# Soft mixture-of-experts block: an expert's second product for two batches side by side in the full array, in groups of four

## Chip, cores and metric

The kernel runs on one NeuronCore of a Trainium2 chip. The metric is device time in microseconds (us) of one execution. Three timed runs of the kernel before gave 1167.07, 1167.43 and 1168.63 us; the median is 1167.43 us. All data are fp32.

## The reference

Sixteen batches of 100 tokens, width 256, pass through a cross attention (16 heads of 16, 361 context tokens each) and then through a soft mixture of 16 experts with 64 slots each. Only the second half matters here:

```python
logits  = einsum('bnd,esd->bnes', x, se)
dispatch = softmax(logits, axis=1)                 # over the tokens
combine  = softmax(logits.reshape(b, n, -1), -1)   # over all 16 * 64 slots
slots = einsum('bnd,bnes->besd', x, dispatch)
gate  = gelu(einsum('besd,edf->besf', slots, Wg) + bg)
up    = einsum('besd,edf->besf', slots, Wu) + bu
eout  = einsum('besf,efo->beso', gate * up, Wd) + bd
out   = x + einsum('bns,bso->bno', combine, eout)  # slots of all experts flattened
```

Per expert, Wg and Wu are 256x512, Wd is 512x256; each is 512 KB.

## The kernel before

**Groups.** The batches go through in groups of 2, 2, 4, 4 and 4 (`GROUPS`). For each group all weights of the 16 experts are streamed in again (80 expert passes, number k = 16 g + e), into six slots of `w_all`. `load_weights` (L1266) issues the next load of a fixed list on SyncE's queue whenever `give_back` (L1282) returns a slot, and with each Wd also that expert's bias `bd`, broadcast to 64 rows: the even expert of a pair has rows 0 to 63 of the tile `bd_bc`, the odd one rows 64 to 127.

**Attention.** `units` works batch by batch: scores (L785) and exponentials (L810) on TensorE in tiles of 32 rows, the product with the values (L833) in tiles of 32 columns, and around them VectorE and ScalarE steps (L790, L801, L818).

**Dispatch.** `dispatch_quarter(g, p, q)` (L927) takes a pair p of batches and a quarter q of the experts (four experts, 256 slots). The logits `lg` have slots on the partitions: 128 partitions are two experts of 64 slots. `copies` (L962) brings them to the tile `lg_all`; they are kept there and later become the combine weights. After the softmax over tokens, two products `sl` (L1033, one per batch) give the slots, transposed, and VectorE (i = 0, L1045) and ScalarE (i = 1, L1048) write them, scaled, into `ring`, ordered (expert, half of the width, batch, slot) by `slots_of` (L914).

**Experts.** `experts(g)` (L1322) takes expert after expert. In a group of four, T = 4*64 = 256 columns; the hidden width is worked in two parts of two 128-wide chunks. Each part makes `gp` and then `up` (L1347, stationary 128x128 weights, moving 256 slot columns, which lie in one run), ScalarE's gelu gives `ge` (L1358), and VectorE's `hT = (up + bu) * ge` (L1363). So hT has the hidden width on partitions and (chunk, batch, slot) on the columns.

**Second product.** `down(g, e, hts)` (L1287) takes a pair of experts after the first part of the expert that follows (at a group's end, at once). Per two batches it makes one PSUM bank `dn`: for each batch and each of four chunks, the stationary operand is one batch's 64 columns of hT, and the two experts of the pair stand in the two 64-column halves of the array. Rows 0 to 63 of `dn` are thus the even expert, rows 64 to 127 the odd one. One VectorE addition (L1309) over 128 partitions and 512 elements adds the bias and writes `eouts_of`, over the quarter's slots in `ring`. Then both Wd slots are returned.

**Combine.** `combine_quarter(g, q)` (L1208) makes, for each batch, `po` (L1218) as the sum over the quarter's two expert pairs c of `lg_all[.., 2c+i, :]` (stationary) and `eouts[:, c, batch, :]` (moving): 128 partitions hold the two experts' slots, and both operands need them in the same order. VectorE adds it to `acc` (L1229). It is run an expert later than it could be; at a group's end it follows the last `down` at once.

**Order.** All of it is issued in an order fixed in advance: generators yield before each step, and a planner with a model of the engines' times (`Clock`, `ck.pe`, `ck.psum_dve`, `ck.copy`) picks whichever task is ready next, with the experts behind the attention units and some of the dispatches. PSUM has four banks for all `mm_tile` products (L65 on), which are taken in turn.

Of the kernel before, what the change touches and what calls it, by code (L numbers as in the profile page):

```python
# [33 lines left out]
F32 = mybir.dt.float32  # L34
AF = mybir.ActivationFunctionType
ALU = mybir.AluOpType
# [11 lines left out]
P = 128  # L48
# [3 lines left out]
QE = 4  # L52
# [77 lines left out]
def xattn_ffn_kernel(  # L130
# [777 lines left out]
    def quarters_before(g, q):  # L908
# [2 lines left out]
        over = [r for r in range(NQ) if spans[g - 1, r][0] < a1 and a0 < spans[g - 1, r][1]]  # L911
        return max(over, default=-1) + 1

    def slots_of(g, q):  # L914
        n = GROUPS[g]
        return regions[g, q].rearrange("p (e k b s) -> p e k b s", e=QE, k=KD, b=n)

    def eouts_of(g, q):
        return regions[g, q].rearrange("p (e b d) -> p e b d", e=QE // 2, d=D)
# [7 lines left out]
    def dispatch_quarter(g, p, q):  # L927

        b0 = 2 * p

        def gate():
            if any(starts[g] + b0 + i not in out_t for i in range(2)):
                return NEVER
            if (g and combined[g - 1] < quarters_before(g, q)) or not lg_free:
                return NEVER
            return max(seT_t[q // 2], out_t[starts[g] + b0 + 1])

        yield gate, 1, (1.35, 0.6, 1.7)
        lg = mm_tile("lg")
        for c in range(2):  # L940
            for kd in range(KD):
                nc.tensor.matmul(  # L942
                    lg[:, c * 2 * N : (c + 1) * 2 * N],
                    lhsT=seT[:, kd, (2 * q + c) * P : (2 * q + c + 1) * P],
                    rhs=xnTs[g][:, kd, b0 * N : (b0 + 2) * N],
                    start=kd == 0,
                    stop=kd == KD - 1,
                )
        t = ck.pe(800, ck.bank())
        lgv = lg[:, : 4 * N].rearrange("p (c n) -> p c n", n=N)  # L950
        slot = lg_free.pop(0)
        lgs = lg_all[:, slot]
        mx = two.tile([P, 4], F32, tag="mx", name="d_mx")
        if len(exps) < 2:
            exps.append(const.tile([P, 4, P], F32, name=f"d_ex{len(exps)}"))
            nc.gpsimd.memset(exps[-1][:, :, N:], 0.0)
        exs = exps[turn[0] % 2]
        turn[0] += 1
        ex = exs[:, :, :N]
        sm = two.tile([P, 4], F32, tag="sm", name="d_sm")  # L960

        def copies(t):  # L962
            nc.scalar.copy(lgs, lgv)
            return ck.copy(400, t)

        def maxima(src, t):
            nc.vector.tensor_reduce(mx, src, AX.X, ALU.max, negate=True)
            return ck.run("DVE", 0.6, t)

        def exponentials(src, t):  # L970
            for i in range(4):
                nc.scalar.activation(
                    ex[:, i],
                    src[:, i],
                    AF.Exp,
                    bias=mx[:, i : i + 1],
                    accum_out=sm[:, i : i + 1],
                )
                t = ck.act("exp", 130, t)
            return t  # L980

        copied = g or q
        if copied:
            tl = copies(t)
            ck.free(tl)
            t = maxima(lgs, tl)
        else:
            t = exponentials(lgv, maxima(lgv, t))
            tl = copies(0.0)
            ck.free(tl)  # L990
        yield t, 0, (0.0, 0.8, 0.0)
        if copied:
            t = exponentials(lgs, t)
            yield t, 0
        nc.vector.reciprocal(sm, sm)  # L995
        t = ck.run("DVE", 0.18, t)
        late = nc.gpsimd if g else nc.vector
        late.tensor_tensor(ex, ex, sm.unsqueeze(2).to_broadcast([P, 4, N]), ALU.mult)  # L998
        t = ck.run("POOL", 0.95, t) if g else ck.run("DVE", 0.6)

        def dispatch():
            disp_sb = two.tile([P, 2, 256], F32, tag="disp", name="disp")
            disp = disp_sb[:N]
            td = t
            if g >= BY_DVE:
                src = exs.rearrange("p (c i) n -> p i c n", c=2)
                dst = disp_sb.rearrange("p i (c a s) -> p i c a s", c=2, a=4)
                for a in range(4):
                    for tb in range(4):
                        if tb % 2 == 0:  # L1010
                            yield td, 0, (0.0, 0.4, 0.0), "aside"
                        toks = slice(32 * tb, 32 * tb + 32)
                        nc.vector.transpose(  # L1013
                            dst[toks, :, :, a, :], src[32 * a : 32 * a + 32, :, :, toks]
                        )
                        td = ck.run("DVE", 0.3, t)
            else:
                tp = mm_tile("d_t")
                for c in range(2):
                    for i in range(2):  # L1020
                        nc.tensor.transpose(  # L1021
                            tp[:N, i * 256 + c * P : i * 256 + (c + 1) * P],
                            ex[:, 2 * c + i, :],
                            ident,
                        )
                nc.scalar.copy(disp.rearrange("n i s -> n (i s)"), tp[:N])
                td = ck.copy(512, ck.run("PE", 0.45, t, ck.bank()))
                ck.free(td)
            for i in range(2):
                yield td, 1, (0.87, 0.4, 0.4)  # L1030
                sl = mm_tile("sl")
                for kd in range(KD):
                    nc.tensor.matmul(  # L1033
                        sl[:, kd * 256 : (kd + 1) * 256],
                        lhsT=xns[g][:, b0 + i, kd * P : (kd + 1) * P],
                        rhs=disp[:, i, :],
                        start=True,
                        stop=True,
                    )
                t2 = ck.pe(512, td, ck.bank())  # L1040
                for kd in range(KD):
                    dst = slots_of(g, q)[:, :, kd, b0 + i, :]
                    srcv = sl[:, kd * 256 : (kd + 1) * 256].rearrange("p (e s) -> p e s", s=S)
                    if i == 0:
                        nc.vector.tensor_scalar(dst, srcv, ng_c[kd], nb_c[kd], ALU.mult, ALU.add)  # L1045
                        t2 = ck.psum_dve(256, t2)
                    else:
                        nc.scalar.activation(  # L1048
                            dst, srcv, AF.Identity, bias=nb_c[kd], scale=ng_c[kd]
                        )  # L1050
                        t2 = ck.copy(256, t2)
                ck.free(t2)
                slot_t[g, q] = max(slot_t.get((g, q), 0.0), t2)
            slots_left[g, q] -= 1
            left[g] -= 1

        yield t, int(g < BY_DVE), (0.45, 0.0, 0.6)
        yield from dispatch()

        yield tl, 0, (0.0, 0.8, 0.0)  # L1060
        if (g, p) not in tops:
            tops[g, p] = [two.tile([P, 2, N], F32, tag="top", name="top"), 0, 0.0]
        top = tops[g, p]
        if top[1]:
            nc.vector.tensor_tensor(top[0], top[0], lgs[:, 0:2], ALU.max)
            nc.vector.tensor_tensor(top[0], top[0], lgs[:, 2:4], ALU.max)
            top[2] = ck.run("DVE", 0.8, tl)
        else:
            nc.vector.tensor_tensor(top[0], lgs[:, 0:2], lgs[:, 2:4], ALU.max)
            top[2] = ck.run("DVE", 0.4, tl)  # L1070
        top[1] += 1
        logits[g, p, q] = slot
# [193 lines left out]
    def load_weights():  # L1266
# [7 lines left out]
        nc.sync.dma_start(t, src.rearrange("(k p) f -> p k f", p=P))  # L1274
        weights[k, name] = t
        if name == "wd":
            if k % 2 == 0:
                biases[k // 2] = two.tile([P, D], F32, tag="bd", name="bd_bc")
            rows = slice(S * (k % 2), S * (k % 2) + S)
            nc.sync.dma_start(biases[k // 2][rows], bd[e].partition_broadcast(S))  # L1280

    def give_back(*names):  # L1282
        for n in names:
# [3 lines left out]
    def down(g, e, hts):  # L1287
# [5 lines left out]
        for half in range(n // 2):  # L1293
            yield max(t for h in hts for _, t in h), 1
            dn = mm_tile("dn")
            for i in range(2):
# [12 lines left out]
            nc.vector.tensor_tensor(  # L1309
                eouts_of(g, q)[:, j // 2, 2 * half : 2 * half + 2, :],  # L1310
                dn.rearrange("p (b d) -> p b d", d=D),
                biases[k // 2].unsqueeze(1).to_broadcast([P, 2, D]),
                ALU.add,
            )
            t = ck.psum_dve(512, ck.pe(2048, ck.bank()))
            ck.free(t)
            done_t[g, q] = t
        give_back((k, "wd"), (k + 1, "wd"))

    HALVED = (1,)  # L1320

    def experts(g):  # L1322
# [4 lines left out]
        for e in range(E):  # L1327
# [3 lines left out]
            for part in range(FC // FB):  # L1331
# [3 lines left out]
                for kind in range(2):  # L1335
# [5 lines left out]
                    for f, fc in enumerate(fcs):  # L1341
# [4 lines left out]
                        for kd in range(KD):  # L1346
                            nc.tensor.matmul(  # L1347
                                ps[:, f * T : (f + 1) * T],
                                lhsT=w[:, kd, fc * P : (fc + 1) * P],
                                rhs=slots_of(g, q)[:, j, kd].rearrange("p b s -> p (b s)"),  # L1350
                                start=kd == 0,
                                stop=kd == KD - 1,
                            )
# [19 lines left out]
                hts.append((hT, t))  # L1373
                if part == 0:
                    if e % 2 == 0 and pair:
                        yield from down(g, e - 2, pair)
                        pair = []
                    if e % QE == 1 and e > 1:
                        to_combine.append(q - 1)
# [1 line left out]
                        yield from combine_quarter(g, to_combine.pop(0))  # L1381
            give_back((k, "wg"), (k, "wu"))
            pair.append(hts)
        yield from down(g, E - 2, pair)
        for q in to_combine + [NQ - 1]:
            yield from combine_quarter(g, q)

# [205 lines left out]
```

## Time and profile before

| | |
|---|---|
| median of three runs | 1167.43 us |
| span of the profiled execution, first to last instruction | 1165.9 us |
| profiled execution, total time apart from the span | not listed; the span is 1.5 us below the median, 1.2 us below the fastest run |
| TensorE busy / VectorE / ScalarE / GpSimd | 1151.4 / 664.6 / 569.4 / 153.7 us |
| TensorE clock granted | 1.00 in every stretch |
| DMA engines busy, data moved | 39.6% by the main queue, 144.84 MB |

The profiled execution has these stretches (us from the span's start): 0 to 97 before the first second product, 97 to 240 and 240 to 440 mostly groups 0 and 1, 440 to 766 group 2 with the attention of groups 3 and 4 in between, 766 to 973 group 3, 973 to 1166 group 4. A busy line of the profile has: source line, engine, operation, tile written <- tiles read, shapes, count, then busy us and mean ns of one, then idle time before it and what ended that. "PE" is a matmul, "PEld" a load of the stationary operand. Each fp32 product of the source is two matmul instructions in the trace. A timeline line has: start us, length us, engine, line, operation, tiles, shapes, count; in it like neighbours are merged. A matmul's length includes its way through the array (0.38 us for 256 columns), while the next one starts earlier; so rates are read from start to start.

### The profile page before, as it was taken

To read this page: it belongs to the slowest core of one execution; us is meant where nothing else is said; L and a number is where in the kernel's file an instruction comes from. 1 tells how busy PE (TensorE), PEld (TensorE's weight loads), DVE (VectorE), ACT (ScalarE), POOL (GpSimd) and SP (SyncE) were. 2 spreads that over 40 slices of the span, in tenths; PEclk is the share of its full clock that TensorE was granted. 3 is DMA by queue.
4 is the path that set the end of the run, shared out by engine and by line. 5 is a ranking of instruction groups with operands and counts; after the bars stand their busy time and mean duration, and the time that the engine had idled before them with its cause. 6 is when DMAs were issued, how large, how long until landed. Compare 5 with 4: busy or idle time off the path is not lost.

```text
span 1165.9 us, 24315 instructions
## 1 busy us (share of the span) xinstructions
PE 1151.4 (99%) x9769; PEld 893.5 (77%) x9769; DVE 664.6 (57%) x1646; ACT 569.4 (49%) x1131; POOL 153.7 (13%) x257
## 2 busy tenths in 40 slices
PE   8899999999999999999999999999999999999998
PEld 6588878787788777777777767787788878777876
DVE  5755546576644678744575765668634456544222
ACT  3556555576454757545545655564433336413110
POOL 3110121013000223300100100031200002002000
PEclk9999999999999999999999999999999999999999
DMA  5415665533467412333521421343443344345441
GB/s 135 136 39 168 204 216 165 161 103 124 140 215 235 116 56 57 72 114 114 134 80 44 119 89 37 114 128 113 136 150 130 113 150 127 114 132 171 134 129 55
DMA packets 138588, 144.84 MB, mean 124 GB/s; under 512 B 45050, under 2 KB 97228, under 8 KB 138476
## 3 DMA queue, kind: packets, MB, share of 16 engines
q1 hardware_dynamic: 137258, 141.50, 39.6%
q8 instruction: 77, 1.26, 0.4%
q0 software_dynamic: 496, 1.12, 0.3%
q10 hardware_dynamic: 722, 0.67, 0.2%
q14 instruction: 35, 0.29, 0.1%
HBM read 141.60 MB, written 1.66 MB: 123 GB/s over the span
## 4 chain that ended last, share of the span: by engine, by line
PE 95%; DVE 2%; DMA 2%; SPq 0%; issue 0%; ACT 0%; POOL 0%; DVEq 0%; ACTq 0%
PE dn L1300 20%; PE gp L1347 19%; PE up L1347 19%; PE sl L1033 5%; PE po L1218 5%; PE at L810 4%; PE at L785 4%; PE v_ps L673 4%; PE lg L942 3%; PE k_ps L613 3%; PE cx L833 3%; DVE mxp L790 1%; PE o_ps L726 1%; PE q_ps L538 1%; PE at L1400 1%; PE d_t L1021 1%
## 5 line engine op out<-in xcount | busy, mean ns | idle before, releaser
L1347 PE MATMUL gp<-ring,w_all 128*128 128x256 f32 (+1 forms) x1280 | 249.1, 341 | 0.5 <-DMA w_all<-in_L_ffn_Wg_dram 0.5
L1347 PE MATMUL up<-ring,w_all 128*128 128x256 f32 (+1 forms) x1280 | 247.9, 340 | 0.0
L1363 DVE SCALAR_TENSOR_TENSOR hT<-up,parT,ge 128x256 f32<-128x256 f32 (+1 forms) x320 | 119.2, 422 | 208.0 <-PE up L1347 157.5
L1300 PE MATMUL dn<-w_all,hT 128*64 128x256 f32 x2048 | 232.1, 382 | 0.0
L1358 ACT ACTIVATE ge<-gp,parT 128x256 f32<-128x256 f32 (+1 forms) x320 | 116.9, 429 | 230.8 <-PE gp L1347 230.1
L1347 PEld LDWEIGHTS gp<-ring,w_all 128*128 128x128 f32 x1280 | 204.5, 191 | 27.9 <-issue 7.3
L1347 PEld LDWEIGHTS up<-ring,w_all 128*128 128x128 f32 x1280 | 204.9, 191 | 21.5 <-issue 1.1
L1300 PEld LDWEIGHTS dn<-w_all,hT 128*64 128x64 f32 x2048 | 142.6, 137 | 78.0 <-issue 7.9
L790 DVE TENSOR_REDUCE mxp<-at 100x4 f32<-100x1444 f32 x64 | 106.2, 1659 | 28.5 <-PE at L785 27.8
L1309 DVE TENSOR_TENSOR ring<-dn,bd_bc 128x512 f32<-128x512 f32 x64 | 44.3, 692 | 131.1 <-PE dn L1300 130.9
L1358 ACT ACT_TABLE_LOAD x71 | 91.1, 1283 | 34.0 <-PE gp L1347 29.5
L818 ACT ACTIVATE aT<-at 121x1200 f32<-121x1200 f32 x64 | 74.9, 1170 | 37.8 <-PE at L810 34.9
L1013 DVE STREAM_TRANSPOSE disp<-d_ex 32x128 f32<-32x128 f32 x256 | 77.4, 302 | 4.6
L717 POOL TENSOR_TENSOR cxs<-cxs,rs 128x100 f32<-128x100 f32 x63 | 25.0, 396 | 381.6 <-DVE rs L714 322.3
L818 ACT ACT_TABLE_LOAD x43 | 55.2, 1283 | 24.1 <-DVE q L801 12.6
L998 POOL TENSOR_TENSOR d_ex<-d_ex,d_sm 128x400 f32<-128x400 f32 x28 | 23.9, 857 | 297.5 <-DVE d_sm L995 297.5
L1033 PE MATMUL sl<-disp,xn 100*128 100x256 f32 x256 | 62.9, 388 | 0.1
L1048 ACT ACTIVATE ring<-sl,parT 128x256 f32<-128x256 f32 x64 | 32.6, 559 | 56.6 <-PE sl L1033 56.6
L1218 PE MATMUL po<-ring,lg_all 128*100 128x256 f32 x256 | 59.7, 383 | 0.0
L810 PEld LDWEIGHTS at<-q,kT 32*121 32x121 f32 x1344 | 40.6, 180 | 19.3 <-issue 7.0
L842 ACT COPY cxs<-cx 128x100 f32<-128x100 f32 x64 | 15.6, 243 | 81.1 <-PE cx L833 80.3
L1033 PEld LDWEIGHTS sl<-disp,xn 100*128 100x128 f32 x256 | 46.7, 190 | 9.5 <-issue 2.5
(165 smaller groups left out, 1323.6 us busy)
## 6 DMA issues: line engine op xcount, KB each, us to landing
w_all<-in_L_ffn_Wg_dram SPq DMA_DIRECT2D x80, 512.0 KB
w_all<-in_L_ffn_Wu_dram SPq DMA_DIRECT2D x80, 512.0 KB
w_all<-in_L_ffn_Wd_dram SPq DMA_DIRECT2D x80, 512.0 KB
bd_bc<-in_L_ffn_bd_dram SPq DMA_DIRECT2D x80, 64.0 KB
c_sb<-in_ctx_dram SPq DMA_DIRECT2D x96, 44.0 KB
acc<-in_x_dram SPq DMA_DIRECT2D x7, 200.0 KB
out_dram<-acc SPq DMA_DIRECT2D x7, 200.0 KB
ring<-n_L_ffn_slot_embeds_dram POOLq DMA_DIRECT2D x1, 1024.0 KB, 7.7
```

The source lines that it names most:

```text
L673: nc.tensor.matmul(ps[: KC + 1, :D], lhsT=cT[:, kd, c * KC : c * KC + KC + 1], rhs=w_sb["wv"][:, kd, :], start=kd == 0, stop=kd == KD - 1,)
L785: nc.tensor.matmul(self.at[:N, r, :S2], lhsT=self.q[rows], rhs=self.k[rows], start=True, stop=True)
L790: nc.vector.tensor_reduce(mxv[:, :, m : m + 1], self.at[:N, :, :S2], AX.X, ALU.max, negate=True)
L810: nc.tensor.matmul(self.at[: KC + 1, r, c * N : (c + 1) * N], lhsT=self.k[rows, c * KC : c * KC + KC + 1], rhs=self.q2[rows], start=True, ...
L818: nc.scalar.activation(self.aT[: KC + 1], self.at[: KC + 1, :, : 3 * N], AF.Exp)
L1013: nc.vector.transpose(dst[toks, :, :, a, :], src[32 * a : 32 * a + 32, :, :, toks])
L1033: nc.tensor.matmul(sl[:, kd * 256 : (kd + 1) * 256], lhsT=xns[g][:, b0 + i, kd * P : (kd + 1) * P], rhs=disp[:, i, :], start=True, stop=True,)
L1218: nc.tensor.matmul(pos[i][:N, :D], lhsT=lg_all[:, slot, 2 * c + i, :], rhs=eouts_of(g, q)[:, c, 2 * p + i, :], start=c == 0, stop=c == 1,)
L1300: nc.tensor.matmul(dn[S * x : S * x + S, i * D : (i + 1) * D], lhsT=hts[x][fc // FB][0].rearrange("p (f b s) -> p f b s", f=FB, s=S)[:, fc ...
L1347: nc.tensor.matmul(ps[:, f * T : (f + 1) * T], lhsT=w[:, kd, fc * P : (fc + 1) * P], rhs=slots_of(g, q)[:, j, kd].rearrange("p b s -> p (b ...
L1358: nc.scalar.activation(ge[:, cols], ps[:, cols], AF.Gelu, bias=col(8, e, fc))
L1363: nc.vector.scalar_tensor_tensor(out=hT[:, cols], in0=ps[:, cols], scalar=col(NPAR, e, fc), in1=ge[:, cols], op0=ALU.add, op1=ALU.mult,)
```

## The change

It applies to groups of four only (`crossed`). Groups of two are computed as before.

- `copies`: for the second pair of batches (p = 1) the logits' upper and lower 64 partitions change places on the way to `lg_all`, with two copies of 64 partitions in place of one of 128. Everything after (softmax, dispatch, combine weights) then has the two experts of each 128 the other way round for these batches.
- The slots of a quarter lie in `ring` as (expert pair c, half of the width, y, batch in pair, slot): y = 0 and 2 are the first pair of batches' even and odd expert, y = 1 and 3 the second pair's odd and even expert. `expert_slots` reads an expert's 256 columns as (batch in pair, y, slot): four runs of 64, of which the even expert's y are 0 and 3, the odd one's 1 and 2.
- So 128 neighbouring columns of hT are one batch of each pair side by side, and for the odd expert the second pair comes first. `crossed_down` makes one bank `dn` per expert with a 128-column stationary operand; its two evictions write 64 partitions each, to where `eouts` has that expert for that pair.
- Each Wd slot is returned after its expert's products, and `bd` is broadcast to 128 rows per expert, in four tiles in place of two.

```diff
+    def crossed(g):
+        return GROUPS[g] == 4
...
+    def crossed_slots(g, q):
+        return regions[g, q].rearrange("p (c k y b s) -> p c k y b s", c=2, k=KD, y=4, b=2)
+
+    def expert_slots(g, q, j, kd):
+        if not crossed(g):
+            return slots_of(g, q)[:, j, kd].rearrange("p b s -> p (b s)")
+        own = slice(1, 3) if j % 2 else slice(0, 4, 3)
+        return crossed_slots(g, q)[:, j // 2, kd, own].rearrange("p y b s -> p b y s")
...
         def copies(t):
+            if crossed(g) and p:
+                nc.scalar.copy(lgs[:S], lgv[S:])
+                nc.scalar.copy(lgs[S:], lgv[:S])
+                return ck.copy(400, ck.copy(400, t))
             nc.scalar.copy(lgs, lgv)
             return ck.copy(400, t)
...
-                    dst = slots_of(g, q)[:, :, kd, b0 + i, :]
-                    srcv = sl[:, kd * 256 : (kd + 1) * 256].rearrange("p (e s) -> p e s", s=S)
+                    srcv = sl[:, kd * 256 : (kd + 1) * 256]
+                    if crossed(g):
+                        dst = crossed_slots(g, q)[:, :, kd, p::2, i, :]
+                        srcv = srcv.rearrange("p (c x s) -> p c x s", c=2, s=S)
+                    else:
+                        dst = slots_of(g, q)[:, :, kd, b0 + i, :]
+                        srcv = srcv.rearrange("p (e s) -> p e s", s=S)
...
         if name == "wd":
+            if crossed(k // E):
+                biases[k] = two.tile([P, D], F32, tag="bd", name="bd_bc", bufs=4)
+                nc.sync.dma_start(biases[k], bd[e].partition_broadcast(P))
+                return
             if k % 2 == 0:
-                biases[k // 2] = two.tile([P, D], F32, tag="bd", name="bd_bc")
+                biases[k] = two.tile([P, D], F32, tag="bd", name="bd_bc", bufs=4)
             rows = slice(S * (k % 2), S * (k % 2) + S)
-            nc.sync.dma_start(biases[k // 2][rows], bd[e].partition_broadcast(S))
+            nc.sync.dma_start(biases[k - k % 2][rows], bd[e].partition_broadcast(S))
...
+    def crossed_down(g, e, hts):
+        k = g * E + e
+        q, j = divmod(e, QE)
+        for x in range(2):
+            yield max(t for h in hts for _, t in h), 1
+            dn = mm_tile("dn")
+            w = weights[k + x, "wd"]
+            for i in range(2):
+                for fc in range(FC):
+                    at = (fc % 2 * 2 + i) * P
+                    nc.tensor.matmul(
+                        dn[:, i * D : (i + 1) * D],
+                        lhsT=hts[x][fc // 2][0][:, at : at + P],
+                        rhs=w[:, fc, :],
+                        start=fc == 0,
+                        stop=fc == FC - 1,
+                    )
+            t = ck.pe(2048, ck.bank())
+            for half in range(2):
+                rows = slice(S * half, S * half + S)
+                p = half ^ x
+                nc.vector.tensor_tensor(
+                    eouts_of(g, q)[rows, j // 2, 2 * p : 2 * p + 2, :],
+                    dn[rows].rearrange("p (b d) -> p b d", d=D),
+                    biases[k + x][rows].unsqueeze(1).to_broadcast([S, 2, D]),
+                    ALU.add,
+                )
+                t = ck.psum_dve(512, t)
+            ck.free(t)
+            done_t[g, q] = t
+            give_back((k + x, "wd"))
...
-                                rhs=slots_of(g, q)[:, j, kd].rearrange("p b s -> p (b s)"),
+                                rhs=expert_slots(g, q, j, kd),
...
-                        yield from down(g, e - 2, pair)
+                        yield from (crossed_down if crossed(g) else down)(g, e - 2, pair)
...
-        yield from down(g, E - 2, pair)
+        yield from (crossed_down if crossed(g) else down)(g, E - 2, pair)
```

More of the change, by code (lines that the diff above doesn't have):

```diff
@@ L1311, in down @@
                 dn.rearrange("p (b d) -> p b d", d=D),
-                biases[k // 2].unsqueeze(1).to_broadcast([P, 2, D]),
+                biases[k].unsqueeze(1).to_broadcast([P, 2, D]),
                 ALU.add,
```

## The prediction

> **What bounds the kernel now.** I read the page first: its shares, its 40 slices and its groups.
>
> ```profile
> span 1165.9 us, 24315 instructions
> PE 1151.4 (99%) x9769; PEld 893.5 (77%) x9769; DVE 664.6 (57%) x1646; ACT 569.4 (49%) x1131; POOL 153.7 (13%) x257
> ...
> PEclk9999999999999999999999999999999999999999
> ...
> L1300 PE MATMUL dn<-w_all,hT 128*64 128x256 f32 x2048 | 232.1, 382 | 0.0
> ...
> L1309 DVE TENSOR_TENSOR ring<-dn,bd_bc 128x512 f32<-128x512 f32 x64 | 44.3, 692 | 131.1 <-PE dn L1300 130.9
> ```
>
> TensorE has work 99% of the time at the full clock, in groups 2 to 4 (440 to 1166 us) idle for 0.6 us and the last 4. VectorE is busy 64, 56 and 40% in the stretches of groups 2, 3 and 4 (table of windows). So only what shortens TensorE's own sequence, or makes it wait, can move the end. The second product is 232 us of it, but the busy time can't tell what one product costs, since ends are modelled. I therefore went to the timeline of TensorE and read starts. Group 4, one `down`:
>
> ```profile
> 1131.77 1.89 PE L1347 MATMUL up<-ring,w_all 128*128 128x256 f32 x8
> ...
> 1133.59 7.13 PE L1300 MATMUL dn<-w_all,hT 128*64 128x256 f32 x64
> ...
> 1140.64 2.00 PE L1347 MATMUL gp<-ring,w_all 128*128 128x256 f32 x8
> ...
> 1142.47 1.89 PE L1347 MATMUL up<-ring,w_all 128*128 128x256 f32 x8
> ```
>
> Between full products, starts are 1.726 us apart per 8 instructions (gp at 776.11, up at 777.84, gp at 779.56): 0.216 us each. The 64 half-width `dn` instructions start in pairs, 7 ns and then 209 ns apart: again 0.216 us per pair. **The two halves of the array already run side by side, so full tiling gains nothing per column:** 32 full instructions will take the 32 x 0.216 = 6.91 us that 32 pairs take.
>
> What the half tiling does cost stands at its borders. From the first `up` (1131.77) to the second (1142.47) are 10.70 us; the work between is 8 + 32 + 8 slots of 0.2158 = 10.36. The other **0.34 us** are: 0.09 before the first `dn` (1131.77 + 1.73 = 1133.50, start 1133.59), 0.05 after its first pair (260 instead of 209 ns), 0.10 before `gp`, 0.10 after gp's first instruction (hence 2.00 instead of 1.89). None of it appears between full products.
>
> In group 2 the attention's 32-row and 32-column products stand around `dn`, and they pay borders of their own:
>
> ```profile
> 676.69 0.89 PE L810 MATMUL at<-q,kT 32*121 32x100 f32 x24
> 677.51 3.67 PE L1300 MATMUL dn<-w_all,hT 128*64 128x256 f32 x32
> 681.12 0.87 PE L785 MATMUL at<-kT,qp 32*100 32x361 f32 x8
> 681.91 0.72 PE L833 MATMUL cx<-aT,vpad 120*32 120x100 f32 x24
> 682.57 1.99 PE L1347 MATMUL gp<-ring,w_all 128*128 128x256 f32 x8
> ```
>
> Here `dn` would be a full product between two 32-row ones. Entering a full product from 32-row or 32-column work costs 0.13 or 0.11 plus 0.10 after its first instruction (this gp's 1.99), leaving it for them 0.09; `dn` now pays 0.13 or 0.11, then 0.05, then 0.10. Such a place loses 0.05.
>
> **The change, part by part.**
>
> *Borders.* I went through all 34 separate stretches of `dn` in groups 2 to 4 with these prices, neighbours as they are now:
> - full product on both sides, 18 stretches (10 in group 3, 8 in group 4): 0.345 each, 0.323 before `po`; together 3.39 + 2.75 = 6.14 us.
> - full on one side only, 13 in group 2: 0.15 each where it leads into 32-row work (9 of them, one 0.21), 0.05 to 0.10 where it comes from `cx` into a single transpose (4); together 1.76 us.
> - neither, 3 in group 2: -0.05 each, -0.14 us.
>
> Sum: **7.75 us saved**, if the order stays.
>
> *Evictions.* 24 pairs of experts had two evictions of 128 x 512; now four of 64 x 512. Partitions do not make them cheaper: additions of 200 elements take 439 ns on 128 partitions (L1066), 381 on 64 (L1156), 433 on 32 (L1157). So 48 more at 0.692 = 33.2 us of VectorE, 11.1 per group, which brings it to 67, 61 and 46% there. Inside a group these lie beside the following products; the combine that reads them comes an expert later, and `dn`'s bank is asked for again only after three other products. If that cover were gone, all 33 us would stand on the path.
>
> *Where the cover is gone: a group's end.* There `po` follows `dn` at once.
>
> ```profile
> 1151.20 7.13 PE L1300 MATMUL dn<-w_all,hT 128*64 128x256 f32 x64
> 1151.38 0.88 DVE L1363 SCALAR_TENSOR_TENSOR hT<-up,parT,ge 128x256 f32<-128x256 f32 x2 [2.58 <-PE up L1347]
> 1154.92 0.69 DVE L1309 TENSOR_TENSOR ring<-dn,bd_bc 128x512 f32<-128x512 f32 x1 [2.67 <-PE dn L1300]
> ...
> 1158.26 3.70 PE L1218 MATMUL po<-ring,lg_all 128*100 128x256 f32 x16
> 1158.38 0.69 DVE L1309 TENSOR_TENSOR ring<-dn,bd_bc 128x512 f32<-128x512 f32 x1 [2.76 <-PE dn L1300]
> ```
>
> Before, the first half's eviction was long done and `po` for the first pair of batches ran while the second half was evicted. Now both pairs of batches need the last expert's two evictions, and the first pair's comes second (for the odd expert, rows 0 to 63 are the second pair). The wait: an eviction starts 0.45 us after the last `dn` instruction starts; two in a row take about 0.61 + 0.69 (two hT in a row: 400 ns start to start at 484 each, so 84 overlap), and TensorE starts 0.055 us after (as L810 after L801): 1.81 us. Of that, 0.65 is covered: the last `dn` slot and the two `po` instructions that read the quarter's first expert pair. **1.16 us** of wait, with 14 `po` products and everything after them queued behind it on TensorE. At group 4's end nothing can fill it. At group 3's end (`dn` to `po` at 969.38 directly) I charge it in full, though the planner, which knows of the later evictions, may put dispatch products there. At group 2's end a `cx` stands between, and about 0.3 is left. Sum **2.6 us lost**.
>
> *Swapped logits.* 12 quarters (3 groups, p = 1) get a second copy: 0.49 us each (L963), 5.9 us of ScalarE at 55% and less, and 0.49 later for the maximum and all after. The slots are used a group later, and TensorE's list of waits (9.8 us in all) has no wait for slots in groups 2 to 4: nothing.
>
> *Strided slots.* gp and up now read four runs of 64 instead of one of 256, in 1536 instructions. No matmul of this trace reads more than one run. Below: 0, a gain has no reason. Above: a run priced like an instruction of its own. 128 columns take 0.112 us and 256 take 0.216, so 8 ns per start, three more starts, 24 ns: 36.9 us. The nearest rows for runs of 64 are the writers of these slots: L1048 writes 4 x 64 in 559 ns, while one-run writes with the same two column operands take 436 (100 elements, L758) and 649 (361, L639), which puts 256 at 563. No price; I take 0.
>
> *Weights and biases.* The even expert's Wd slot returns half a `down` (3.5 us) earlier; the load issues, as many as before and in the same order on SyncE, are delayed by nothing. The 48 biases grow from 64 to 128 KB, 3.1 MB on 144.84, with DMA at 31 to 41% in these groups: nothing. They are four tiles deep, two pairs, as before.
>
> *Stationary loads.* The trace shows loads of 128 columns at 0.19 us beside matmuls of 0.216 without a gap (8 gp in 1.73 us), so `dn` in this form costs no more. The Trainium skill, "TensorE: Matmul & The Clock Gate", Part 3, What overlaps and what doesn't, speaks against the change: it lets a load overlap a running matmul only if the row groups differ, which full-height loads never do. By it, 768 exposed loads of 0.19 would cost 146 us; gp and up contradict it here. "SBUF — State Buffer", Specifications (TRN2), charges reads that use too little of a 16-byte line; runs of 256 bytes use whole lines, so by it the strided read costs nothing, which no run here shows.
>
> **Sum.** 1165.9 - 7.75 + 2.6 = 1160.8 us of span, 5.1 less; the median stands 1.5 above the span, so **1162.3 us**. The planner sees one more eviction per `dn` and will order some steps differently; one border more or less is 0.2 to 0.35 us, so I allow 2.5 either way.
>
> **Rivals.**
> - *Forecast, 1159.8 to 1165.0:* borders gone, group ends paid. 0.64. With it goes the case that the planner fills the ends: up to 7.75, 1159.7; 0.06.
> - *VectorE gives it back, 1165.1 to 1169.7:* not only the ends wait. For it: VectorE works its list in the order issued and stands still behind `dn` (130.9 us of its idle time), and in group 2 the chain maximum, transpose, addition (L790, L801) runs through it; L810 already waited 3.5 us for L801. Each eviction that hits such a chain costs up to 0.61 us, 16 places in group 2 make 9.8; 5 hits (3 us) bring the change within the bound. Against: at 67% there is room, and in group 2's 326 us TensorE is idle for 0.6 in all (table of windows: busy 325.38), because the planner puts other products into such chains. Seven hits give 4.2, 1166.5; 0.18.
> - *Strided reads, slower:* at L1347, 1536 instructions. From 3.3 ns each the gain is gone, from 4.9 ns the kernel is slower by over 0.2%; at 8 ns it is 1162.3 + 12.3 = 1174.6, at 24 ns 1199. For it: no such row. Against: the writers above. 0.10.
> - *It doesn't do what it says:* `dn` still with gaps of its own, as if the 128-column loads weren't hidden. From 10 ns per instruction (768) slower. gp and up speak against it. 0.02.
>
> **Chances and range.** What a measurement of this kernel can tell from no change is about 0.2%, 2.3 us. Faster 0.64 + 0.06 = 0.70, same 0.18, slower 0.12. For 8 in 10 the range runs from 1159.5 (all borders, filled ends) to 1168.0 (most of the VectorE case); the strided case, whose bound lies far out, and a little of the VectorE case stay outside, 0.16 in all.
>
> **What would show it.** `dn` as 128*128 instructions 0.216 us apart, 768 of them in groups 2 to 4 beside 512 of the old form; in group 4 gp to up to `dn` to gp without 0.09 or 0.10 in between, and 10.36 us where 10.70 stood; gp of four runs with unchanged starts (else the strided rival); L1309 at 0.69 us for 64 partitions; a wait of about 1.2 us of `po` on VectorE's L1309 successor at the end; no growth of TensorE's waits for VectorE in group 2 (else the second case). Wrong would be the forecast if full `dn` kept a border cost, or if the waits at the ends were over 2 us each.

## The result, and the profile after

The changed kernel takes 1172.22 us (median of five runs, 1170.85 to 1173.79) against 1167.43: 1.0034 times the time before, 95% interval 1.0021 to 1.0047. It is slower by 4.8 us; the forecast was 1162.3, 5.1 faster. The profiled execution has a span of 1170.4 us, 4.5 more than before.

Page of the changed kernel (in a group line: busy us, mean ns of one, then idle time before it):

```profile
span 1170.4 us, 22908 instructions
...
PE 1148.8 (98%) x9001; PEld 934.9 (80%) x9001; DVE 697.3 (60%) x1694; ACT 560.6 (48%) x1131; POOL 153.5 (13%) x257
...
PEclk9999999999999999999999999999999999899999
...
L1358 PE MATMUL dn<-w_all,hT 128*128 128x256 f32 x768 | 171.8, 380 | 0.0
...
L1369 DVE TENSOR_TENSOR ring<-dn,bd_bc 64x512 f32<-64x512 f32 x96 | 66.1, 689 | 76.6 <-PE dn L1358 75.8
```

TensorE has 768 instructions fewer and VectorE 33 us more, as the diff says. What had not been there is the 8 in the clock's row near its end, and idle time of TensorE. The table of its waits after 440 us (engine, line and tile that waited <- what ended it: total us, times, longest):

```profile
PE sl L1051 <- DVE disp L1031: 4.6, 1, 4.6
PE po L1241 <- DVE ring L1369: 2.1, 2, 1.1
```

These are two of its three lines; the third, 0.4 us, is a wait of `q_ps` that the kernel before has too, with 0.3, as the only line of its table. The two lines shown are two different things. `po` waits for evictions at the ends of groups, as forecast. The 4.6 us are a wait for slots in group 4. TensorE's timeline there, changed kernel:

```profile
1002.63 1.89 PE L1407 MATMUL gp<-ring,w_all 128*128 128x256 f32 x8
1004.36 1.89 PE L1407 MATMUL up<-ring,w_all 128*128 128x256 f32 x8
1010.88 3.75 PE L1051 MATMUL sl<-disp,xn 100*128 100x256 f32 x8 [4.64 <-DVE disp L1031]
1014.43 2.30 PE L956 MATMUL lg<-xnT,seT 128*128 128x200 f32 x8
1016.57 1.67 PE L1407 MATMUL gp<-ring,w_all 128*128 128x256 f32 x7
```

The slots' product `sl` of the second quarter, second pair of batches, waits for VectorE's transposes of `disp`; the experts of that quarter cannot begin without it. When it does run, `sl` takes 3.75 us and `lg` 2.30. Before the change the same product came early, 12 us ahead of the `gp` that reads it (at 1012.61), and both ran at their usual lengths:

```profile
1000.89 1.89 PE L1033 MATMUL sl<-disp,xn 100*128 100x256 f32 x8
1002.62 1.52 PE L942 MATMUL lg<-xnT,seT 128*128 128x200 f32 x8
1003.97 1.89 PE L1347 MATMUL gp<-ring,w_all 128*128 128x256 f32 x8
```

The longer instructions are the clock's. Table of windows of the changed kernel, 1009.00 to 1016.02 us (PE, PEld, DVE, ACT and POOL busy, then the granted clock, 0.51, the DMA share and GB/s):

```profile
1009.00:1016.02 7.02, 5.14 (x13) 4.45 (x14) 4.50 (x15) 1.02 (x2) 0.00 (x0) 0.51 0.11 43
```

In the clock's own records it stands at 0.5 from 1009.19 for 6.83 us. From the start of `sl` to the `gp` that follows are 5.69 us; before, with the same instructions, 3.08: 2.6 us lost to the clock.

Is VectorE simply too busy to transpose in time? Its timeline says no (the time in brackets is idle time ahead of the instruction, and what ended it):

```profile
992.47 1.39 DVE L1369 TENSOR_TENSOR ring<-dn,bd_bc 64x512 f32<-64x512 f32 x2 [2.51 <-PE dn L1358]
993.89 1.24 DVE L1031 STREAM_TRANSPOSE disp<-d_ex 32x128 f32<-32x128 f32 x4
995.93 1.39 DVE L1369 TENSOR_TENSOR ring<-dn,bd_bc 64x512 f32<-64x512 f32 x2 [0.79 <-PE dn L1358]
997.35 1.25 DVE L1031 STREAM_TRANSPOSE disp<-d_ex 32x128 f32<-32x128 f32 x4
...
1002.90 0.88 DVE L1423 SCALAR_TENSOR_TENSOR hT<-up,parT,ge 128x256 f32<-128x256 f32 x2 [1.30 <-PE up L1407]
1003.81 0.62 DVE L1031 STREAM_TRANSPOSE disp<-d_ex 32x128 f32<-32x128 f32 x2
...
1009.49 1.90 DVE L1031 STREAM_TRANSPOSE disp<-d_ex 32x128 f32<-32x128 f32 x6
```

Between 988 and 1007 us VectorE idles five times for TensorE, 5.9 us in all, while transposes wait further down its list, which come two or four at a time between evictions and `hT`. The order put them there.

**Where the 4.5 us of span come from**, by comparing starts of the two traces step by step: borders -7.75 (the order is another, so this is the forecast's figure; against experiment 2 below, which has this order and the old products, they are 7.5); group ends +2.4 (1.21 twice); the late slots +4.8 of wait, from start to start, and +2.6 of clock; two waits at the end of group 1 (`d_t` for GpSimd's `d_ex` 1.1 us, `sl` for ScalarE's `disp` 0.7) +1.8; the start +0.7, among it another 3.41 us of half clock at 43 us that cost 1.6 and that two other runs, 1170.85 and 1171.02, don't have by their mean clock (0.997 against 0.995). Sum +4.55, which is the 4.5 within its rounding. The fall at 43 us is chance: both kernels run the same TensorE sequence up to 420 us. Without it the changed kernel takes about 1170.9 us, 3.5 more than before.

### The profile page after: what moved, and what is told of

It reads as the page before. It is cut to its first block, busy times and chain, and to the rows that moved or that the text cites. A ratio compares the mean times of both kernels' runs of the same rounds, so it can differ in the third digit from the quotient of the medians.

```text
span 1170.4 us, 22908 instructions
## 1 busy us (share of the span) xinstructions
PE 1148.8 (98%) x9001; PEld 934.9 (80%) x9001; DVE 697.3 (60%) x1694; ACT 560.6 (48%) x1131; POOL 153.5 (13%) x257
## 3 DMA queue, kind: packets, MB, share of 16 engines
q8 instruction: 71, 1.16, 0.4%
## 4 chain that ended last, share of the span: by engine, by line
PE 96%; DVE 2%; ACT 1%; issue 0%; DMA 0%; POOL 0%; SPq 0%; DVEq 0%; ACTq 0%
PE gp L1407 19%; PE up L1407 19%; PE dn L1358 14%; PE sl L1051 5%; PE dn L1327 5%; PE po L1241 5%; PE at L810 5%; PE at L785 4%; PE lg L956 4%; PE v_ps L673 4%; PE k_ps L613 3%; PE cx L833 3%; PE o_ps L726 1%; PE q_ps L538 1%; PE at L1460 1%; DVE mxp L790 1%
## 5 line engine op out<-in xcount | busy, mean ns | idle before, releaser
L1358 PE MATMUL dn<-w_all,hT 128*128 128x256 f32 x768 | 171.8, 380 | 0.0
L1358 PEld LDWEIGHTS dn<-w_all,hT 128*128 128x128 f32 x768 | 144.7, 190 | 20.4 <-issue 0.6
L1369 DVE TENSOR_TENSOR ring<-dn,bd_bc 64x512 f32<-64x512 f32 x96 | 66.1, 689 | 76.6 <-PE dn L1358 75.8
L1327 PE MATMUL dn<-w_all,hT 128*64 128x256 f32 x512 | 58.8, 382 | 0.0
```

What stands on the lines that cost most here:

```text
L1327: nc.tensor.matmul(dn[S * x : S * x + S, i * D : (i + 1) * D], lhsT=hts[x][fc // FB][0].rearrange("p (f b s) -> p f b s", f=FB, s=S)[:, fc ...
L1358: nc.tensor.matmul(dn[:, i * D : (i + 1) * D], lhsT=hts[x][fc // 2][0][:, at : at + P], rhs=w[:, fc, :], start=fc == 0, stop=fc == FC - 1,)
L1369: nc.vector.tensor_tensor(eouts_of(g, q)[rows, j // 2, 2 * p : 2 * p + 2, :], dn[rows].rearrange("p (b d) -> p b d", d=D), biases[k + x][r ...
```

## The experiments

The planner that fixes the order is told costs by the code: `ck.psum_dve(512, t)` for each eviction, `ck.copy(400, t)` for each copy of the logits. The diff adds a second of both. A kernel's real instructions and what the planner is told can thus be varied separately. Two theories: **ORDER**, the told costs made another order, in which the slots come late; **VECTORE**, the extra evictions themselves delay VectorE's chains, in whatever order.

**1. new_products_old_order.** The changed kernel, the planner told as before.

```diff
-                return ck.copy(400, ck.copy(400, t))
+                return ck.copy(400, t)
...
-                t = ck.psum_dve(512, t)
+                if half:
+                    t = ck.psum_dve(512, t)
```

> The changed kernel, but the planner is told what it was told before (one eviction per dn bank, one copy of the logits), so TensorE's instructions come in the order of the kernel before; all evictions and copies are still made. Theory ORDER (the loss is the order that the planner made from the new costs: the slots of group 4's second quarter come late, TensorE waits 4.6 us and then runs at half clock): borders saved 7.75, group ends lost 2.6, so about 1162.3 us (1161 to 1164), clock 1.00 from 100 us on, no TensorE wait over 1.5 us in groups 2 to 4. Theory VECTORE (the 33 us of extra evictions themselves delay what TensorE waits for): 1168 us or more, with a wait of several us on VectorE in groups 2 to 4.

1165.78 us, ratio 0.9989 (0.9980 to 0.9998), span 1164.3. TensorE's sequence is now that of before but for the `dn`, and the wait of 4.6 us is gone, as ORDER has it; yet most of the gain is missing. Its waits after 760 us:

```profile
PE po L1241 <- DVE ring L1369: 2.9, 3, 1.6
PE sl L1051 <- DVE disp L1031: 0.8, 1, 0.8
PE o_ps L726 <- DVE cxs L721: 0.6, 1, 0.6
```

With the same order, every step can be compared with before: the borders give 7.75 (1.62, 3.39 and 2.75 in groups 2, 3, 4), the three group ends take 0.39 + 1.81 + 1.21 = 3.4, and four places inside groups where TensorE now waits for VectorE take 0.50 + 0.42 + 0.86 + 0.89 = 2.7. Together -1.65. From group 2's first product to TensorE's last start the trace is 1.0 shorter, so 0.6 of smaller steps are not in this list; another 0.4 lies ahead of group 2, and the span is 1.6 shorter.

Two of these items are not the evictions'. The 0.50 stands at 449 us, ahead of group 2's first `dn`, where second copies of the logits are the only instructions that are new; the chain that ends there runs through one (L979, 0.49 us at 438.79), then the maximum `d_mx`, VectorE's list and a transfer. And at the end of group 3 the evictions come late because VectorE, which works in the order of its list, stands at a `d_mx` that waits for the second copy:

```profile
967.95 0.57 DVE L985 TENSOR_REDUCE d_mx<-lg_all 128x4 f32<-128x400 f32 x1 [4.11 <-ACT lg_all L979]
968.43 1.38 DVE L1369 TENSOR_TENSOR ring<-dn,bd_bc 64x512 f32<-64x512 f32 x2
```

They start 1.01 us after the last `dn` starts, where 0.42 pass at the end of group 4: hence 1.81 in place of 1.21.

**2. old_products_new_order.** The opposite: the kernel before, the planner told what the changed kernel tells it.

```diff
+            if GROUPS[g] == 4 and p:
+                t = ck.copy(400, t)
...
+            if n == 4:
+                t = ck.psum_dve(512, t)
```

> The kernel before, but the planner is told the costs of the changed one (two evictions per dn bank and two copies for the second pair in groups of four), so TensorE's instructions come in the changed kernel's order; nothing else is computed or added. Theory ORDER: 3.5 to 4.6 us of wait before the sl products of group 4's second quarter, half clock after it (about 2.5 us more), about 1.8 us at the end of group 1: 1173 to 1178 us. Theory VECTORE: as before, 1166.5 to 1168.5 us.

1177.00 us, ratio 1.0086 (1.0073 to 1.0100), span 1173.8. No instruction is new here, and no eviction is split, but the wait stands in the same place with the same length, and the clock falls to 0.5 for 6.83 us again:

```profile
1012.86 3.75 PE L1035 MATMUL sl<-disp,xn 100*128 100x256 f32 x8 [4.64 <-DVE disp L1015]
1016.41 2.57 PE L942 MATMUL lg<-xnT,seT 128*128 128x200 f32 x8
```

ORDER is confirmed: the order alone costs 10.0 us in the medians. It also brings the two waits at the end of group 1 (1.1 and 0.7).

**3. old_order_split_evictions.** The kernel before and its order; only the evictions are really split in two.

```diff
+            parts = [slice(0, S), slice(S, P)] if n == 4 else [slice(0, P)]
+            for rows in parts:
+                nc.vector.tensor_tensor(
+                    eouts_of(g, q)[rows, j // 2, 2 * half : 2 * half + 2, :],
+                    dn[rows].rearrange("p (b d) -> p b d", d=D),
+                    biases[k // 2][rows].unsqueeze(1).to_broadcast([rows.stop - rows.start, 2, D]),
+                    ALU.add,
+                )
...
```

> The kernel before in its own order; only each eviction of dn in groups of four is made as two of 64 partitions, 33 us more VectorE work that the planner is not told of. Theory ORDER: 1167 to 1169 us, the work lies beside TensorE. Theory VECTORE: 1171 us or more, with waits of TensorE on VectorE that the kernel before doesn't have.

1170.31 us, ratio 1.0026 (1.0016 to 1.0035), span 1167.6: between the two expectations. In an order that doesn't know of them, the 48 evictions cost 1.7 us of span (3.3 in the medians; the profiled execution was one of its fastest), at three of the four places of 1 (+0.45 at 501 us, +0.71 at 819, +0.70 at 961). The fourth, at 449 us, is missing here, and so is the second copy of the logits. VECTORE is real, but a third as large as the order.

**4. new_products_old_order_first_pair_first.** As 1, and the odd expert's bank is evicted first pair first.

```diff
-            for half in range(2):
+            for p in range(2):
+                half = p ^ x
...
```

> As the first of these, and for the odd expert the eviction that the first pair of batches needs is made first. If the wait at a group's end is for the second of two evictions, it shrinks by about 0.6 to 0.7 us at the ends of groups 3 and 4: 1.2 to 1.4 us faster than without it, about 1161 us. If that wait has another cause: no difference.

1163.76 us, ratio 0.9971 (0.9960 to 0.9981): 2.0 us better than 1, more than the 1.2 to 1.4 expected. Start by start, 0.39, 0.57 and 0.70 of it stand at the ends of groups 2, 3 and 4, and 0.25 at 501 us. From the start of the last `dn` to the third `po` are 1.17 us where 1 has 1.86 and before 0.82. The mechanism at the group ends is the one forecast.

**5 and 6. told_two_evictions_one_copy, told_one_eviction_two_copies.** The changed kernel with only one of the two added costs told; the instructions are all there.

```diff
-                return ck.copy(400, ck.copy(400, t))
+                return ck.copy(400, t)
```

> The changed kernel with all its work; the planner is told both evictions of a dn bank, but one copy of the logits as before. By the planner's own clock its order ends 6.9 us earlier than the changed kernel's. If the late slots of group 4's second quarter need both new costs in the plan: no such wait, 1164 to 1168 us. If the told evictions alone make them: 1170 to 1173 us, with the wait of over 4 us.

1163.64 us, ratio 0.9972 (0.9962 to 0.9983).

```diff
-                t = ck.psum_dve(512, t)
+                if half:
+                    t = ck.psum_dve(512, t)
```

> The changed kernel with all its work; the planner is told both copies, but one eviction per dn bank. By the planner's own clock its order ends 4.6 us earlier than the changed kernel's. If the late slots need both costs in the plan: no such wait, 1165 to 1169 us. If the told copies alone make them: 1170 to 1173 us, with the wait of over 4 us.

1168.74 us, ratio 1.0015 (1.0006 to 1.0024). Neither has the wait of 4.6 us: it takes both told costs. The told copy alone brings the waits at the end of group 1. Told of the evictions, the planner also hides them: of the waits inside groups that 1 shows, 5 has one, of 0.6 at 449.9 us (0.50 from start to start). The table puts it down to VectorE, but as in 1 its chain runs through the second logits copy (L979, at 439.71). So the copies that really run cost 5 half a microsecond, although the planner was told of one.

**7. wait_filled_with_products.** The changed kernel; while the planner sees `sl` unready, TensorE makes products of the identity that nothing reads.

```diff
+            if begun and group == len(GROUPS) and not streams["units"] and now + 2.0 < ready[first]:
+                holding.append(1)
+            if holding and now + 0.2 < ready[first]:
+                warm_up()
+                continue
...
```

> The changed kernel in its own order; only where the planner sees TensorE wait more than 2 us in group 4, it now issues 18 products of a constant that nobody reads (about 4 us), so that TensorE is busy while it waits. If the clock falls because TensorE stood still: granted clock 1.00 after it, and the 5.1 us that ran at half clock take 2.5: 1169 to 1170.5 us. If the clock fell for another reason: as the changed kernel, 1171 to 1173 us.

1171.47 us, ratio 1.0025 (1.0016 to 1.0034). The median hides two sets: four of eleven executions have no low clock at all (mean 1.0) and take 1167.68 to 1168.85; the others take 1170.08 to 1171.91. The profiled one belongs to the second set:

```profile
1008.38 4.18 PE L1460 MATMUL at<-ident 128*128 128x128 f32 x36
1013.18 1.97 PE L1051 MATMUL sl<-disp,xn 100*128 100x256 f32 x8 [0.62 <-DVE disp L1031]
1014.98 1.52 PE L956 MATMUL lg<-xnT,seT 128*128 128x200 f32 x8
```

The clock doesn't fall at the filled wait, and `sl` and `lg` have their usual lengths. But it falls in this execution at 427.14 us, for 6.83 us, beside the two waits at the end of group 1. So the fall at the late slots follows from the wait. The executions without any fall are 2.4 us below those of the changed kernel with one (1168.6 against 1170.85 and 1171.02), near the 2.6 worked out above. That every execution of the second set fell at 427 us is not shown, only that this one did.

**8. old_order_last_bank_by_batch.** As 4, and the last expert of a group makes one bank per batch, so that evictions begin half a bank earlier.

```diff
+            split = e == E - 2 and x == 1
+            for part in range(2 if split else 1):
+                dn = mm_tile("dn")
+                those = (part,) if split else (0, 1)
+                for i in those:
...
```

> Changed products with the planner told what it was before, the first pair evicted first, and for the last expert of each group one dn bank per batch, so that the first batch is evicted while the second is made. If po waits at a group's end for the evictions and nothing else, about 1.1 us at the end of group 3 and 0.5 to 0.7 at the end of group 4 go: 1161.5 to 1162.8 us, against 1163.8 without it. Otherwise 1163.8.

1163.19 us, ratio 0.9965 (0.9953 to 0.9978). `po` at the end starts without a wait (0.65 us from the last `dn` to the third `po`); one wait of 0.8 stays, at the end of group 3, where VectorE stands at the `d_mx` that waits for the second logits copy, as in 1. So `po` doesn't wait for the evictions and nothing else there. The step from 4 is 0.6 us, less than the 1.0 to 2.3 expected, and the intervals overlap.

**9. told_copies_last_bank_by_batch.** Both edits of 8, and the planner told as in 5: two evictions, one copy. Against 8:

```diff
-                    if p == 0 or False:
+                    if p == 0 or True:
                         t = ck.psum_dve(256 * n, t)
```

> The changed kernel with the planner told of two evictions per second product and one logits copy, the first pair's half evicted first, and the last expert of each group in one bank per batch. ORDER: the order with those costs gave 1163.64 us with VectorE waits of 3.1 us at the group ends; the other two edits took 2.0 and another 0.6 us off the order of the kernel before. The same here would be about 1161.0; the planner's order moves again with any edit, so 1160.5 to 1163. VECTORE (the extra evictions cost 2 to 3 us in any order and the order is chance): 1163 to 1165, no better than the version with the order of the kernel before (1163.2).

1159.17 us, ratio 0.9924 (0.9911 to 0.9938), span 1157.1: 8.2 us faster than before, and better than both theories had it. TensorE's waits after 440 us are two, 0.6 (the one at 449 us in 1 and 5) and 0.3 (`v_ps` at 585 us, behind two evictions). From the first product of group 2 to the end are 718.4 us; before, 726.2: 7.8 less.

**10 and 11. old_products_told_two_one_copy, old_products_best_order.** Is that gain the products' or a lucky order's? The kernel before, with the planner told as in 5 and as in 9. TensorE's sequence is that of 5, or 9, apart from the `dn`. The edits, of 10 and then of 11:

```diff
             t = ck.psum_dve(512, ck.pe(2048, ck.bank()))
+            if n == 4:
+                t = ck.psum_dve(512, t)
             ck.free(t)
```

```diff
-            t = ck.psum_dve(512, ck.pe(2048, ck.bank()))
-            ck.free(t)
+            parts = 2 if n == 4 and e == E - 2 and half else 1
+            for _ in range(parts):
+                t = ck.pe(2048 // parts, ck.bank())
+                for _ in range(n // 2):
+                    t = ck.psum_dve(512 // parts, t)
+                ck.free(t)
```

> The kernel before with its old products, in the order that the planner makes when told of two evictions per bank and one logits copy: TensorE's sequence is that of told_two_evictions_one_copy (1163.64 us) apart from the second products. PRODUCTS (the gain there comes from the new products, which took 1.2 us off in the order of the kernel before and 4.8 us in the order of the changed kernel): 1165 to 1168.5. ORDERGAIN (that order alone is better than the one before, and the products bring nothing): 1162 to 1164.5.

1167.44 us, ratio 1.0003 (0.9994 to 1.0012).

> The kernel before with its old products in the order of told_copies_last_bank_by_batch (1159.17 us), TensorE's sequence being the same apart from the second products. There no wait of the new products is left, so the borders' full 7.75 us should stand between the two. PRODUCTS: 1166 to 1168, about the kernel before. ORDERGAIN: under 1163, so that half or more of the 8.2 us is the order's.

1166.73 us, ratio 0.9996 (0.9987 to 1.0004), span 1164.9. Those orders by themselves are no better than the one before, so the products bring the gain. TensorE's timeline in 11, and the same place in 9:

```profile
1106.34 1.89 PE L1351 MATMUL up<-ring,w_all 128*128 128x256 f32 x8
1108.16 7.13 PE L1300 MATMUL dn<-w_all,hT 128*64 128x256 f32 x64
1115.22 1.99 PE L1351 MATMUL gp<-ring,w_all 128*128 128x256 f32 x8
1117.05 1.89 PE L1351 MATMUL up<-ring,w_all 128*128 128x256 f32 x8
```

```profile
1101.25 7.07 PE L1361 MATMUL dn<-w_all,hT 128*128 128x256 f32 x32
1108.16 1.89 PE L1412 MATMUL gp<-ring,w_all 128*128 128x256 f32 x8
1109.89 1.89 PE L1412 MATMUL up<-ring,w_all 128*128 128x256 f32 x8
```

From `dn` to the second `up`: 8.89 us in 11, 8.64 in 9; with the 0.09 ahead of `dn` that is the 0.34 of the forecast.

The four orders together, medians in us:

| order of | old products | new products | difference |
|---|---|---|---|
| the kernel before | 1167.02 | 1165.78 | -1.2 |
| the changed kernel | 1177.00 | 1172.22 | -4.8 |
| two evictions, one copy told | 1167.44 | 1163.64 | -3.8 |
| the same, last bank by batch, first pair first | 1166.73 | 1159.17 | -7.6 |

The rows come from several sets of runs; the kernel before has medians of 1167.02 to 1167.43 in them. The products are faster in every order. Down the column of old products, where they play no part, the order of the changed kernel costs 10 us and the other three agree within 0.7.

## Why the prediction was wrong, point by point

- **Borders, 7.75 us: right.** In the same order they are 7.75 (1), and 9 against 11 shows 7.5 from group 2's first product to the end (718.4 against 725.9) with no group-end wait left; 9's two waits, which 11 doesn't have, take 0.9 of it, so the 33 stretches of that order give 8.4. The Trainium skill, "TensorEngine Tiling (Array Packing)", Key Properties, says that changing the tiling mode drains TensorE. The 0.34 us per `dn` between full products agree with that: they go when the mode no longer changes. That a drain is what takes them is not shown.
- **Rate of the new product, strided slots, stationary loads: right.** In group 4 of the changed kernel the starts are 1.72 + 6.91 + 1.73 us apart, 10.36 from `up` to `up`, with four runs of 64 columns read by `gp` and `up`:

```profile
1135.72 1.89 PE L1407 MATMUL up<-ring,w_all 128*128 128x256 f32 x8
1137.44 7.07 PE L1358 MATMUL dn<-w_all,hT 128*128 128x256 f32 x32
1144.35 1.89 PE L1407 MATMUL gp<-ring,w_all 128*128 128x256 f32 x8
1146.08 1.89 PE L1407 MATMUL up<-ring,w_all 128*128 128x256 f32 x8
```

  The strided rival and "it doesn't do what it says" are out.
- **An eviction's price: right.** 689 ns on 64 partitions, 692 on 128.
- **Group ends, 2.6 us: right in kind.** At the end of group 4 the third `po` starts 1.86 us after the last `dn`, 1.81 forecast, so that the wait is 1.21 where 1.16 stood. In the old order the sum is 3.4 (group 3's end 1.81, with the logits copy in it), in the changed kernel 2.4:

```profile
1158.81 2.97 PE L1358 MATMUL dn<-w_all,hT 128*128 128x256 f32 x13
1161.62 0.59 PE L1241 MATMUL po<-ring,lg_all 128*100 128x256 f32 x2
1163.26 3.27 PE L1241 MATMUL po<-ring,lg_all 128*100 128x256 f32 x14 [1.05 <-DVE ring L1369]
```

- **"Inside a group these lie beside the following products": too generous by 2 to 3 us** in an order that doesn't know of the evictions (1: 2.2 us at three places; 3: 1.7 of span, 3.3 in the medians). The VectorE rival had the mechanism. In 9, with the evictions told, one wait of 0.3 is left of it.
- **Swapped logits, "nothing": too small for the copies that run, wrong for the copies that are told.** "The slots are used a group later" was a misreading: in the kernel before, the slots that group 4's `gp` reads at 1012.61 are made at 1000.89, in group 4 itself. The copies that run cost 0.5 us at 449 us in 1, 5 and 9, and most of 0.6 at the end of group 3 in 1; in the changed kernel no wait of theirs shows: against 2, which has its order and no second copies, only `po`'s waits are new. The told cost alone brings 1.8 us of waits at the end of group 1 (6), which the prediction, made for groups 2 to 4, did not look at; the dispatches of group 2 run there.
- **The step that failed is in the sum:** "The planner sees one more eviction per `dn` and will order some steps differently; one border more or less is 0.2 to 0.35 us, so I allow 2.5 either way." A new order was expected, but priced by the borders it might add. What it can do is place a whole chain late: a slots' product that stood 12 us ahead of its reader became the last thing the reader waited for. That cost 4.8 us, 2.6 more of halved clock, and 1.8 at the end of group 1: 9.2 us, over three times the allowance. The bound should have been worked out from what a late `sl` costs, since 16 transposes of 0.30 us, VectorE's list between them, stand ahead of each.
- **A small term, 1.5 us from span to median:** every execution on record takes 1.7 to 1.9 us more than its own span. The 1.5 came from setting one execution's span against the median of others.

Open: which of the planner's choices first moved the transposes back. It rations such side steps by how far VectorE's planned clock runs ahead of TensorE's (2.5 us, `BACKLOG`), so the told evictions probably leave them less room; but 5 tells the evictions too and has no late slots, so the two costs act together, and I did not isolate one step.

## What to carry to other kernels

Where a planner fixes the order, a change has two prices, that of its instructions and that of the order made from the costs it reports; measure them apart, by telling the planner the old costs with the new instructions and the new costs with the old instructions. A wait in a new order is not bounded by the cost that was added: look for the product whose result a whole stage needs, and for how early it stood before. And an accumulation bank that two consumers need should be evicted in the order in which they come, in pieces at the place where nothing else can cover it: with the planner's costs mended as well, those two edits turned +4.8 us into -8.2.

## What the runs showed of the hardware that was not expected

**A wait of 4.6 us halves TensorE's clock for longer than it lasts.** In the changed kernel and in 2, the granted clock falls to 0.5, 2.9 and 3.5 us into the wait, and stays there for 6.83 us, over 5 of them after work has begun again; the price was 2.6 us on top of the wait in the changed kernel and 2.9 in 2. Filling the wait with products (7) kept the clock at 1.0 there. The Trainium skill, "TensorE: Matmul & The Clock Gate", Part 1, says that the array falls to half its rate after an idle window of about 3.4 us; the 6.83 here is twice 3.41. A wait that long does not stand ahead of all falls: one of 3.41 us began at 43 us in the changed kernel's profiled execution, one at 29 us in 5's and one of 6.83 at 427 us in 7's, with no wait of TensorE over 1.4 us near them; and 7's other executions differ among themselves.

The clock's records show one thing more: in all 13 traces the granted clock changes only at whole steps of 3.413 us, counted from its first rise. The step ahead of the fall in group 4 has 0.47 us of matmuls in the changed kernel and none in 2. So it matters how a wait lies to these steps. The two waits at the end of group 1 stand in four traces. In 7 they leave matmuls 1.67 us of one step (423.73 to 427.14 us), and the clock falls at its end; in the changed kernel, 2 and 6 the poorest step there has 2.15, 2.43 and 2.49 us, and it doesn't fall. How little is too little does not come out: the falls at 43 and 29 us follow steps with 2.19 and 2.35 us, and one with 1.49 us (8, 1156.12 to 1159.54) brought none. Which short waits bring it down stays open.

**A run of 64 columns costs nothing as a moving operand.** Four runs of 64 fp32 columns pass at the rate of one run of 256: 0.216 us from start to start, 1536 instructions.
